# Order of SyncE's queue in an adaLN layer: the spread of 1/std one slot later, the loads of x behind the norm

## The chip, the cores and the metric

The kernel runs on one core of a Trainium2 chip. The metric is the device time of one execution in microseconds (us), as a median over runs. The engines are named as the profile does: PE (TensorE matmuls; PEld its weight loads), DVE (VectorE), ACT (ScalarE), POOL (GpSimd), SP (SyncE). SyncE computes nothing here. It issues nearly all DMAs, in the order of the program, and each issue first waits for what that DMA needs.

## The reference

One layer on `x` of shape (4, 2048, 512), float32: a state-space part and a channel-mixing part, each behind a layer norm and with a gate, modulated by a small input `c`. Cut to what matters:

```python
mod = (_silu(c) @ wmod).reshape(4, 6, 1, -1)              # sa, ca, ga, sb, cb, gb
h = _layernorm(x) * (1 + ca) + sa
omega = clip(softplus(h @ W_omega.T + b_omega)); zeta = sigmoid(h @ W_zeta.T + b_zeta)
A, S, d, F = omega**2, 1 / (1 + DT*DT*omega**2), 1 - zeta, h @ W_B.T + b_B
# scan over the 2048 tokens, 2 x 64 states:
z, y = d*(S*z - DT*A*S*y) + F_z,  d*(DT*S*z + S*y) + F_y
x = x + ga * (states @ C.T + h @ D_mat.T)
h = _layernorm(x) * (1 + cb) + sb
xr, xk = (mu * h + (1 - mu) * h_prev_token for mu in (mu_r, mu_k))
x = x + gb * sigmoid(xr @ W_r.T) * (square(relu(xk @ W_k.T)) @ W_v.T)
```

The norm needs a mean and a standard deviation for each of the 8192 tokens. Its scale 1/std multiplies the gate projections token by token, and there the tokens lie along the free dimension. So the kernel needs each unit's 1/std as a row on all 128 partitions.

## The kernel before

**Units and slots.** The tokens are cut into 32 units of 256 tokens. Unit number i belongs to batch row i % 4 and to token stretch i // 4. Four units with the same stretch form a block, and the scan over tokens runs block by block. The main loop (L1205) has one slot per unit. In slot i several units are at different stages:

- `fin[i]` (class `Finish`) does its key product (`key_fast`), its receptance product (`receptance_fast`) and its `value`, and its results go out (L760).
- `fin[i+1]` (`ahead` in the code) gets its direct product with `dg` and the states, its statistics (`stats`, L557 and L559), its norm, and its mixing (`mix`).
- `fin[i+2]` is loaded (`x`, L117; `xt`, L114).
- `gts[i+8]` (class `Gates`) is projected (`project_pieces`, L244), multiplied by its spread 1/std (`multiply`, L252) and delivered to the scan.
- `gts[i+9]` gets its norm: means (L186) and squares (L192) on ScalarE, then 1/std and std on GpSimd (L196 to L198).
- `gts[i+10]` has its two tiles of `x` loaded (`load`, L159; the tiles are called `xs`).

`at = i % 4` is the place of a slot in its block. I call `at == 0` the first slot and `at == 3` the fourth. Slots below i = 4 have a branch of their own that the change does not touch. In the slots from i = 4, the norm's ScalarE work stands between the products of the key multiplication, except in the first slot. There it stands behind `deliver`, almost at the slot's end, because ScalarE also has the scan's functions to do in that slot.

**How a norm reaches the gates.** `send` (L202) writes a unit's std and 1/std from `rs` (SBUF) to a small DRAM tile `st`: 512 numbers, 2 KB. `spread` (L213) reads the row of 1/std back onto all 128 partitions, into `bc`. A spread therefore waits for the landing of its send. The scan reads the rows of std from the same DRAM tiles (`load_std`, L408, in a block's third slot).

**Buffers that matter.** `xs` has three buffers and a unit takes two. So of the two loads for `gts[i+10]` one finds a free buffer, and the other has to wait until the squares of `gts[i+9]` are done. `xt` has three buffers, shared by `fin` and `gts`. `r` (the receptance, and then the result that goes out) has two buffers, one for each half of a unit. The first and second eviction of a receptance product (L666 and L669, both on ScalarE) write the two `r` buffers, so they have to wait until the results of the previous unit have left. The third of the seven receptance products accumulates in the bank that L666 reads, so TensorE waits for L666. `bc` has two buffers.

**What sets the order.** Each engine runs its instructions in the order in which this Python code emits them. The order is written out by hand: `f.emit(products, beside)` emits the seven products of a multiplication and, behind each, the jobs listed for it. For the SyncE queue the order within a slot is therefore the order in which `load`, `send`, `spread`, `fetch` and `value` are called in the code. `fetch("dg", i + 3)` and `fetch("wv", i + 2)` bring a batch row's 1 MB weights back from DRAM (L800).

Of the kernel before, what the change touches and what calls it, by code (L numbers as in the profile page):

```python
# [22 lines left out]
B, T, D, M = 4, 2048, 512, 64  # L23
# [24 lines left out]
def adaln_layer_kernel(ctx: ExitStack, tc: tile.TileContext, x, x_t, c_t, wmod, w_gate, w_b, b_gate, b_f, c_mat, d_mat,  # L48
# [99 lines left out]
    class Gates:  # L148
# [62 lines left out]
        def spread(self, queue=nc.sync):  # L211
            self.bc = p2.tile([P, W], F32, tag="bc", name=f"bc_{self.u.tag}")
            queue.dma_start(self.bc, self.rows[0:1, :].broadcast_to([P, W]))  # L213
# [582 lines left out]
    def fetch(name, i):  # L796

        if 6 <= i < len(fin):
            dst = dg if name == "dg" else wvb
            nc.sync.dma_start(dst[:, i % 2].rearrange("p k d -> p (k d)"), kept[name][i % B])  # L800
# [404 lines left out]
    for i, f in enumerate(fin):  # L1205
        at = i % B
        ahead = fin[i + 1] if i + 1 < len(fin) else None
        if i < 4:
            if i == 3:
                take(100)  # L1210
            fin[i + 2].load()
            gts[i + 10].load()
            f.key()
            if i < 2:
                rows(turn_d[i + 2], turn_c[i + 2])
            if i == 0:
                gts[6].multiply()
                gts[6].deliver(share=2)
            else:
                norm_send(i + 9)  # L1220
            if i == 3:
                gates(11)
            take(6)
            if i == 2:
                sums_s(key_weights, quarters_of(wk, True))
            if i == 3:
                sums_t(receptance_weights, quarters_of(wr))
            ahead.attend(lambda: take(2))
            ahead.normalize()
            turn(turn_v[i])  # L1230
            keep_in_dram("wv", i)
            if i == 3:
                fetch("dg", i + 3)
            if i == 0:
                gts[7].multiply()
                gts[7].deliver(share=2)
                gts[8].norm_dve()
                gts[8].send()
                gts[8].spread()
                gts[9].norm_dve()  # L1240
                gts[9].send()
            if i == 1:
                gates(9)
            if i:
                take(5)
            f.receptance()
            ahead.mix(fin[i + 2].shift)
            if i == 0:
                side += scan(1)
                take(0.1)  # L1250
                take(0.1)
            gts[i + 9].load_t()
            gts[i + 9].spread()
            if i < 3:
                turn_v[i + 1].rows()
            f.value(lambda: take(3 if i == 0 else 4))
            if i < 2:
                turn(turn_d[i + 2], turn_c[i + 2])
                keep_in_dram("dg", i + 2)
                gates(8 if i == 0 else 10)  # L1260
        else:
            if i + 2 < len(fin):
                fin[i + 2].load()
            shares = [0] * 7
            if at < B - 1:
                left = sum(e[1] for e in side if e) if at == B - 2 else 1
                shares = [e * left for e in SHARES[at]]
            scans = [lambda e=e: take_share(e) for e in shares]

            def fill(jobs, n):  # L1270
                for _ in range(n):
                    if jobs:
                        jobs.pop(0)()

            def filler(jobs, n):
                return lambda: fill(jobs, n)

            direct, ends = ahead.attend_pieces() if ahead else ([[], []], [])
            gate = gts[i + 8].project_pieces() if i + 8 < len(gts) else []

            def stats(n, part=None):
                return lambda: ahead.stats(n, part) if ahead else None

            def finish_norm():
                if ahead:
                    ahead.normalize_rest()

            def norm_means():
                if i + 9 < len(gts):
                    gts[i + 9].norm_means()  # L1290

            def norm_squares():
                if i + 9 < len(gts):
                    gts[i + 9].norm_squares()
                    gts[i + 9].send()

            def load_gates():
                if i + 10 < len(gts):
                    gts[i + 10].load()

            if at < B - 1:
                load_gates()
            eight = i in EIGHT
            if not eight:
                f.receptance_sums()

            if not ahead:
                one, other = f.key_fast(), f.receptance_fast((ps1, "pg"))
                f.emit(one[:2])
                for n in range(2, len(one)):  # L1310
                    f.emit(one[n : n + 1])
                    f.emit(other[n - 2 : n - 1])
                    if n == 5:
                        f.relu(1)
                        f.squares(1)
                f.relu(0)
                f.squares(0)
                f.emit(other[5:])
                finish = None
            elif at == B - 1:  # L1320
                take(100)
                take(1)
                load_gates()
                d = direct[0] + direct[1]
                fill(d, 2)
                f.emit(f.key_fast(), {1: [filler(d, 1), norm_means], 7: [filler(d, 1), norm_squares], 6: [filler(d, 1)], 4: [filler(d, 1)],
                            5: [filler(d, 1)], 2: [filler(d, 1)]})
                fetch("dg", i + 3)
                f.relu(0)
                fill(ends, 1)  # L1330
                stats(0)()
                fill(ends, 1)
                stats(1)()
                f.relu(1)
                finish = {1: [filler(gate, 1), lambda: f.squares(0)], 7: [filler(gate, 1)],
                          6: [filler(gate, 1), finish_norm], 4: [filler(gate, 1), lambda: f.squares(1)]}
            else:
                scans[0]()
                d = direct[0] + ends[:1] + direct[1] + ends[1:]
                fill(d, 2)  # L1340

                acts = ([lambda: take(0.1), lambda: take(0.1)], [norm_means, norm_squares])[at > 0]
                acts = acts + [lambda: None] if at != 1 else [lambda: None] + acts
                f.emit(f.key_fast(), {1: [filler(d, 2)], 7: [filler(d, 1), acts[0]],
                                      6: [filler(d, 2), scans[1], acts[1], stats(0)],
                                      4: [filler(d, 2), scans[2], acts[2]], 5: [filler(d, 1), scans[3]],
                                      2: [stats(1, 0)], 3: [stats(1, 1), scans[4]]})
                fetch("dg", i + 3)
                finish = {1: [filler(gate, 1)], 7: [filler(gate, 1), lambda: f.relu(0)],
                          6: [filler(gate, 1), finish_norm],  # L1350
                          4: [filler(gate, 1), scans[5], lambda: f.relu(1), lambda: f.squares(0)],
                          5: [lambda: f.squares(1)]}
            if eight:
                for k in (1, 7, 6, 4, 5):
                    for job in finish.get(k, ()):
                        job()
                f.receptance()
            elif ahead:
                f.emit(f.receptance_fast(), finish)

            def between():
                if not eight:
                    f.sigmoids()
                if i + 2 < len(fin):
                    fin[i + 2].shift()

            if ahead:
                ahead.mix(between)
            else:
                f.sigmoids()  # L1370
            if i + 9 < len(gts):
                gts[i + 9].load_t()
            fill(gate, len(gate))
            if i + 8 < len(gts):
                gts[i + 8].multiply()
                gts[i + 8].deliver()
            if at == 0:
                norm_means()
                norm_squares()
            if i + 9 < len(gts):  # L1380
                gts[i + 9].spread()
            f.value(scans[6], parts=1 if ahead else 2)
            fetch("wv", i + 2)
        if at == B - 1 and i + 8 < len(gts):
            assert not side
            side += scan(i // B + 2)
# [43 lines left out]
```

## Time and profile before

| what | us |
|---|---|
| median of 3 runs | 1166.02 |
| lowest and highest run | 1164.06, 1168.04 |
| the profiled execution, its time | 1167.16 |
| its span in the profile | 1165.3 |
| TensorE busy in that span | 1108.0 |

The profile is of one execution. Its time is 1.86 us more than its span, which is what lies around the program's first and last instruction. A row of the engine view gives, for each engine, its busy time and the number of instructions. The rows of waits read "who waited, on which line, for whom: total us, how often, the longest". A row of the timeline gives start, duration, engine, line, operation, and in brackets how long the engine had been idle before and who ended that. DMA rows of SyncE (SPq) give the time of issue; several issues of one line that follow each other are merged into one row, whose duration then includes the waits between them.

### The profile page before, as it was taken

The page shows a single profiled execution, that of the slowest core. Times are in us where ns is not written, and L with a number is a line of the kernel's source. Part 1 is how long each engine was busy: PE and PEld are TensorE (multiplying, and loading weights), DVE is VectorE, ACT ScalarE, POOL GpSimd, SP SyncE. Part 2 cuts the span into 40 slices and gives each one's busy share as a digit, 9 for nine tenths or more (in the row PEclk, how much of TensorE's full clock was granted, in tenths as well). Part 3 has the DMA queues.
Part 4 walks back from the last instruction along what each step waited for, and adds up shares of the span by engine and source line. Part 5 has one row for each costly group of instructions (what it writes and reads, how often), then busy time and mean ns, then how long its engine had stood idle before and what let it go on. Part 6 is the DMA issues. An engine that isn't in the chain of part 4 may idle for free.

```text
span 1165.3 us, 14897 instructions
## 1 busy us (share of the span) xinstructions
PE 1108.0 (95%) x4772; PEld 747.4 (64%) x4772; DVE 777.8 (67%) x2158; ACT 669.3 (57%) x1380; POOL 188.9 (16%) x389
## 2 busy tenths in 40 slices
PE   7898899999899997999889998999979999999998
PEld 4556566656666665777566675666657765566666
DVE  5796678547576585756857566765867568764444
ACT  1655776638465675556666475656756465435553
POOL 1212201211111122101211111111221011111110
PEclk9889899999899998999999999999989999999999
DMA  9895374540787527883297825967168433443211
GB/s 299 304 153 143 89 161 141 153 158 6 193 177 180 146 64 170 179 167 118 65 257 143 157 76 166 199 177 155 62 165 168 145 127 127 136 145 127 91 55 37
DMA packets 133991, 168.32 MB, mean 144 GB/s; under 512 B 22292, under 2 KB 96788, under 8 KB 126104
## 3 DMA queue, kind: packets, MB, share of 16 engines
q1 hardware_dynamic: 130904, 166.03, 55.9%
q10 hardware_dynamic: 2688, 0.79, 0.3%
q8 instruction: 38, 0.62, 0.3%
q0 software_dynamic: 320, 0.53, 0.2%
q14 instruction: 41, 0.34, 0.1%
HBM read 137.90 MB, written 25.23 MB: 140 GB/s over the span
## 4 chain that ended last, share of the span: by engine, by line
PE 79%; DVE 12%; DMA 4%; ACT 4%; issue 1%; POOL 0%; ACTq 0%; DVEq 0%; POOLq 0%
PE pv_c L754 16%; PE pd_c L538 13%; PE pxr_c L657 8%; PE pxk_c L657 7%; PE pg L244 5%; PE pr_c L739 4%; PE pzk_c L657 3%; PE pzr_c L657 3%; PE pd_c L493 3%; PE pg L234 3%; PE pd_c L470 3%; PE pt_c L594 2%; DMA out_dram<-r_c 2%; PE pyr_c L657 2%; PE pk_c L627 2%; PE pyk_c L657 2%
## 5 line engine op out<-in xcount | busy, mean ns | idle before, releaser
L754 PE MATMUL pv_c<-wvb,act_c 128*128 128x512 f32 (+1 forms) x528 | 225.0, 580 | 0.0
L538 PE MATMUL pd_c<-dg,xt 128*128 128x512 f32 x432 | 206.2, 593 | 0.0
L603 DVE SCALAR_TENSOR_TENSOR mixed_c<-pt_c,prev_f,mixed_c 128x255 f32<-128x255 f32 x256 | 118.1, 481 | 80.9 <-ACT mixed_c L600 80.5
L754 PEld LDWEIGHTS pv_c<-wvb,act_c 128*128 128x128 f32 x528 | 99.6, 190 | 105.5 <-issue 100.1
L600 ACT ACTIVATE mixed_c<-pt_c,mod,now_f 128x256 f32<-128x256 f32 x256 | 130.2, 559 | 19.8 <-DVE mixed_c L603 14.0
L538 PEld LDWEIGHTS pd_c<-dg,xt 128*128 128x128 f32 x432 | 74.6, 191 | 55.9 <-issue 54.2
L244 PE MATMUL pg<-xt,wgb 128*128 128x256 f32 x320 | 89.0, 392 | 6.9 <-DMA xt<-in_x_t_dram 6.9
L478 DVE SCALAR_TENSOR_TENSOR x<-pd_c,rs,x 128x512 f32<-128x512 f32 x64 | 47.6, 745 | 54.0 <-PE pd_c L493 48.7
L657 PE MATMUL pxr_c<-wvb 128*128 128x256 f32 x208 | 58.6, 408 | 23.2 <-ACT r_c L666 23.2
L657 PEld LDWEIGHTS pxk_c<-dg 128*128 128x128 f32 x448 | 58.8, 192 | 25.9 <-issue 24.4
L244 PEld LDWEIGHTS pg<-xt,wgb 128*128 128x128 f32 x320 | 61.0, 197 | 15.8 <-issue 8.0
L463 POOL TENSOR_TENSOR x<-x,d 128x1024 f32<-128x1024 f32 x30 | 70.9, 2362 | 0.0
L557 ACT ACTIVATE xn_c<-x 128x512 f32<-128x512 f32 x44 | 27.7, 628 | 67.7 <-DVE x L478 63.9
L574 ACT ACTIVATE xn_c<-x,mean_c,var_c 128x512 f32<-128x512 f32 x64 | 48.6, 808 | 29.5 <-POOL mean_c L572 29.5
L267 ACT ACTIVATE pre<-g,bias 64x256 f32<-64x256 f32 x56 | 41.5, 742 | 37.6 <-DVE g L252 30.8
L657 PEld LDWEIGHTS pxr_c<-wvb 128*128 128x128 f32 x208 | 41.3, 203 | 31.4 <-ACT r_c L666 25.6
L657 PE MATMUL pxk_c<-dg 128*128 128x128 f32 x448 | 59.1, 275 | 0.0
L675 DVE TENSOR_TENSOR r_c<-r_c,pzr_c 128x256 f32<-128x256 f32 x26 | 10.9, 420 | 69.4 <-PE pzr_c L657 35.9
L493 PE MATMUL pd_c<-cg,y 128*128 128x512 f32 x112 | 56.5, 595 | 0.0
L606 POOL TENSOR_TENSOR mixed_c<-mixed_c,edge_c 128x4 f32<-128x4 f32 x64 | 12.9, 201 | 263.5 <-ACT mixed_c L600 263.4
L757 DVE TENSOR_TENSOR r_c<-pv_c,r_c 128x512 f32<-128x512 f32 (+1 forms) x66 | 44.0, 666 | 9.6 <-PE pv_c L754 9.6
L758 DVE TENSOR_TENSOR r_c<-r_c,x 128x512 f32<-128x512 f32 (+1 forms) x66 | 44.6, 676 | 2.3
(261 smaller groups left out, 2135.4 us busy)
## 6 DMA issues: line engine op xcount, KB each, us to landing
dg<-dg SPq DMA_DIRECT2D x30, 1024.0 KB, 5.8
xt<-in_x_t_dram SPq DMA_DIRECT2D x116, 256.0 KB, 7.5
wvb<-wv SPq DMA_DIRECT2D x26, 1024.0 KB, 5.5
x<-in_x_dram SPq DMA_DIRECT2D x32, 512.0 KB, 6.7
out_dram<-r_c SPq DMA_DIRECT2D x62, 256.0 KB, 2.2
xs<-in_x_dram SPq DMA_DIRECT2D x54, 256.0 KB, 6.8
wvb<-in_wmod_dram SPq DMA_DIRECT2D x5, 1024.0 KB, 8.6
y<-pre SPq DMA_DIRECT2D x64, 64.0 KB, 4.6
```

The lines of the kernel that those rows point to most:

```text
L244: nc.tensor.matmul(self.pg[:, i, :], wgb[:, u.b, k, ts(i, P)], self.xt[:, k, :], start=(k == 0), stop=(k == KC - 1))
L463: engine.tensor_tensor(xt, xt, d0[:, self.u.b, :].unsqueeze(1).broadcast_to([P, NT, D]), ALU.add)
L478: nc.vector.scalar_tensor_tensor(xt, pd, r, xt, ALU.mult, ALU.add)
L493: nc.tensor.matmul(pc, y_of[u.s][:, u.b, ts(n, P)], cg[:, u.b, :], start=start, stop=True)
L538: nc.tensor.matmul(pds[n], self.h[:, k, ts(n, P)], dg[:, self.at, k, :], start=(k == 0), stop=False)
L574: nc.scalar.activation(self.xn[:, n, :], self.x[:, n, :], AF.Identity, bias=self.mean[:, n : n + 1], scale=self.var[:, n : n + 1],)
L600: nc.scalar.activation(m, pt, AF.Identity, bias=mod[:, SB, k, b : b + 1], scale=now_f[:, b, i, k : k + 1])
L603: nc.vector.scalar_tensor_tensor(m[:, 1:], pt[:, : W - 1], prev_f[:, b, i, k : k + 1], m[:, 1:], ALU.mult, ALU.add)
L657: nc.tensor.matmul(to[:, j, :], left[:, k, ts(j, P)], right[:, k, :], start=start and j == k == 0, stop=(k == 1), skip_group_check=True,)
L739: nc.tensor.matmul(pr, mixed[:, 0, k, ts(n, P)], wr[:, k, :], start=(k == 0), stop=(k == KC - 1))
L754: nc.tensor.matmul(pv, act[:, k, ts(n, P)], wvb[:, self.at, k, at], start=(j == 0), stop=(j == KC - 1))
L758: nc.vector.tensor_add(r[:, at], r[:, at], xt[:, n, at])
```

## The change

The program's arithmetic is the same, and so is the order of instructions on TensorE, VectorE, ScalarE and GpSimd. What moves is the place of three kinds of DMA in SyncE's queue, in the slots from i = 4:

- The spread: slot i used to spread `gts[i+9]`, shortly before `value`. It now spreads `gts[i+8]`, the unit that this same slot multiplies, behind the key product. Slot 4 spreads nothing, since slot 3 has spread its unit already.
- The loads of `xs` for `gts[i+10]`: they stood at the slot's start (in the fourth slot behind the scan's last jobs). They now follow the send of `gts[i+9]` directly.
- The send: in the second, third and fourth slot it used to be issued inside the key product, right behind the squares. It now stands behind the key product, and in the second and third slot behind the fetch of `dg`. In the first slot it used to follow the squares, ahead of the spread and of the results; it now stands behind both results of `value`, with the loads behind it.

```diff
             def norm_squares():
                 if i + 9 < len(gts):
                     gts[i + 9].norm_squares()
+
+            def send_load():
+                if i + 9 < len(gts):
                     gts[i + 9].send()
+                load_gates()
 
             def load_gates():
                 if i + 10 < len(gts):
                     gts[i + 10].load()
 
-            if at < B - 1:
-                load_gates()
+            def spread():
+                if 4 < i < len(gts) - 8:
+                    gts[i + 8].spread()
+
             eight = i in EIGHT
...
             elif at == B - 1:
                 take(100)
                 take(1)
-                load_gates()
                 d = direct[0] + direct[1]
                 fill(d, 2)
                 f.emit(f.key_fast(), {...})
+                send_load()
+                spread()
                 fetch("dg", i + 3)
...
                 fetch("dg", i + 3)
+                if at:
+                    send_load()
+                spread()
                 finish = {...}
...
             if at == 0:
                 norm_means()
                 norm_squares()
-            if i + 9 < len(gts):
-                gts[i + 9].spread()
             f.value(scans[6], parts=1 if ahead else 2)
+            if at == 0:
+                send_load()
             fetch("wv", i + 2)
```

## The prediction

> **What bounds the kernel now.** I read the page's first two parts, then the same row per slot, then who ends TensorE's waits, then SyncE's queue.
>
> ```profile
> PE 1108.0 (95%) x4772; PEld 747.4 (64%) x4772; DVE 777.8 (67%) x2158; ACT 669.3 (57%) x1380; POOL 188.9 (16%) x389
> ...
> core 0: us, PE busy (x) PEld busy (x) DVE busy (x) ACT busy (x) POOL busy (x), PEclk, DMA share, GB/s
> 287.10:328.40 41.30, 36.31 (x145) 24.60 (x145) 28.20 (x81) 23.76 (x54) 7.69 (x14) 0.88 0.63 164
> ...
> 529.20:561.30 32.10, 32.10 (x146) 22.33 (x145) 20.69 (x45) 22.44 (x43) 5.24 (x11) 1.00 0.27 90
> 561.30:602.00 40.70, 33.98 (x145) 23.15 (x145) 28.19 (x81) 23.76 (x54) 7.68 (x14) 0.96 0.64 161
> 602.00:634.10 32.10, 32.10 (x145) 22.18 (x145) 25.03 (x92) 20.03 (x45) 5.43 (x11) 1.00 0.81 170
> ```
>
> The windows run from the end of one slot's `value` matmuls to the next one's. TensorE fills a normal slot: 32.1 us busy of 32.1. The second slot of a block does not fit that. The five windows of this kind (287.1, 424.6, 561.3, 698.3, 834.6) last 41.3, 40.4, 40.7, 40.0 and 40.3 us, 42.2 us in all above 32.1 each. 30.1 us of that is idle TensorE (length less busy), the other 12.1 us mostly half clock after it (PEclk 0.88 to 0.96). So these 42.2 us are all that a reordering can win here. Who ends the wait:
>
> ```profile
> PE pxr_c L657 <- ACT r_c L666: 23.2, 5, 6.4
> PE pg L244 <- DMA xt<-in_x_t_dram: 6.9, 3, 3.5
> ...
> ACT r_c L666 <- DMA out_dram<-r_c: 37.9, 5, 8.1
> ...
> SPq L213 <- DMA st<-rs: 196.1, 22, 12.2
> SPq L159 <- ACT xs L192: 172.6, 12, 31.5
> ...
> 533.54 32.09 SPq L159 DMA_DIRECT2D xs<-in_x_dram  x2
> 565.73 0.38 SPq L800 DMA_DIRECT2D dg<-dg  x1
> 566.16 1.23 SPq L114 DMA_DIRECT2D xt<-in_x_t_dram  x2
> 567.88 0.38 SPq L202 DMA_DIRECT2D st<-rs  x1
> 579.24 0.33 SPq L213 DMA_DIRECT2D bc<-st  x1
> 579.65 0.86 SPq L760 DMA_DIRECT2D out_dram<-r_c  x2
> ```
>
> Five times ScalarE cannot write `r` (L666), because the last slot's results still have to leave that buffer. SyncE issues in order: a load of `xs` waits through the whole first slot for the norm, then the spread waits for the send (11.3 us), and only then do the results go, 15 us after VectorE made the second (L758 ended at 564.5). They land at 585.2, L666 starts at 585.25, TensorE at 585.68.
>
> **The change, part by part.** Work on TensorE, VectorE, ScalarE and GpSimd stays, in its order; SyncE's list alone is shuffled.
>
> *The spread a slot later.* Its 1/std was sent a slot earlier and has landed, so SyncE's 196.1 us of waiting go. The results of a first slot then go out when made (561.5 and 564.5) and land some 2.2 us later, ten before `r` is written. The 37.9 us of ScalarE's wait go.
>
> *`dg` and `xt` of a first slot.* Both go up to 20 us earlier; the 6.9 us of TensorE's wait for `xt` go.
>
> *Results first, then send, then loads, at the end of a first slot.* The send still needs GpSimd's 1/std, so it stays at 567.88. Both loads of `xs` now follow it, at about 568.3 and 568.7; before, one was issued 35 us earlier and the other at 565.30. Their reader is the next slot's norm, early in ScalarE's list:
>
> ```profile
> 568.30 0.37 ACT L672 COPY act_c<-pxk_c 128x256 f32<-128x256 f32 x1 [1.38 <-PE pxk_c L657]
> 568.57 0.63 ACT L186 ACTIVATE xs<-xs 128x512 f32<-128x512 f32 x1
> ...
> 572.25 0.63 ACT L557 ACTIVATE xn_c<-x 128x512 f32<-128x512 f32 x1 [2.35 <-DVE x L478]
> ...
> 576.44 0.72 ACT L559 ACTIVATE xn_c<-x,mean_c 128x512 f32<-128x512 f32 x1
> ...
> 585.25 0.37 ACT L666 COPY r_c<-pxr_c 128x256 f32<-128x256 f32 x1 [8.00 <-DMA out_dram<-r_c]
> ```
>
> Queued behind L186 are the statistics of the next unit, the squares, the last eviction of the key product and L666 itself, for which TensorE's third receptance product waits. From L186 to L666 there are 1.34 us (568.57 to 569.91) and 5.00 us (572.25 to 577.25), less 0.21 us of waiting for TensorE: 6.13 us of work, and TensorE resumes 0.43 us after. So the question is X, the time from the send to the landing of the first `xs`.
>
> No `xs` load follows a send in this trace. Nearest are the third slots, where `dg` (1024 KB) follows a send on a queue with little ahead: sends at 339.73, 476.00, 612.98, 749.28 and 885.02; `dg` issued 0.63 to 1.17 us later lands 12.3, 14.0, 13.7, 13.5 and 13.7 us after its issue, thus 13.2, 14.9, 14.4, 14.1 and 14.9 us after the send, mean 14.3. Alone, `dg` takes 5.0 to 5.2 us and an `xs` 2.6; the smaller load is 2.5 us quicker, so X is 11.8 us. From below: a send alone lands after 8.9 us at the earliest, and some 0.7 us of transfer follow: 9.6. From above: the four `std` loads behind the send at 200.13, 256 KB together, landed by 13.2. I take 11.8, the row nearest in place and load.
>
> Here two statements of the Trainium skill pull apart. Its page "DMA: Bandwidth & Descriptors", section "Anatomy of one DMA — SWDGE (gpsimd) path", fits a DMA of that path as 2.0 us plus bytes over 436 GB/s: 2.6 us for 256 KB, which the trace shows on SyncE's queue too when nothing is ahead. By that X is about 3, ScalarE's 2.35 us of slack swallows the wait, and the sum is the full gain of 42 us. The section "Queues, rings and completion order" says that a semaphore's increment lands only after all earlier writes of that DMA engine, and the send's writes are just ahead. It speaks against this change, and the third slots are on its side, with X four times as long. I go by the row.
>
> Per block: L666 can start at send + 11.8 + 6.13, plus 0.17 because the second tile lands some 0.8 us after the first while its activation is ready 0.63 us after. That is send + 18.1. Before it was send + 17.43, 16.65, 17.37, 16.46, 16.76 (L666 at 311.09, 447.83, 585.25, 721.33, 857.94), mean 16.93. The stall is thus kept and grows by 1.2 us: five times, +5.9 us.
>
> *The clock.* The first of the five windows lost 4.2 us beyond its idle time, the others about 2 each, with PEclk 0.88 against 0.92 to 0.96. The page "TensorE: Matmul & The Clock Gate", section "What's actually happening", has the clock halved after an idle window of about 3.4 us and full after a busy one. By that, one cold window per stall costs 1.7 us, 3.6 us less than before's 12.1 over five. By the rows, only the first comes down to the others' 2: -2.0 us. I take the rows.
>
> *Loads and spread of the other slots.* In the second slot the norm is done at send + 16.3 and GpSimd 1.74 us later, so the next send goes at 585.9. Its loads land by 599 and are read at 607.6: no cost. The spread behind them lands between 599.0 (scaled from `dg` for 640 KB ahead and with it) and 602.4 (3.4 us more, since a spread's median landing is 6.0 us where an `xs` alone has 2.6). `multiply` wants it at 599.12 plus the shift, 599.8. VectorE may thus wait up to 2.6 us; ScalarE's 1.79 us of idle time before 604.63 and TensorE's bank, wanted only at 603.5, cover nearly all. I put 0, at most +0.5 per block. In third and fourth slots the spread is out by 627 and 523, wanted at 631 and 526: no cost while sends stay within 4 us of the present.
>
> Sum: +5.9 - 2.0 = +3.9 us. The profiled execution (span 1165.3, time 1167.16) stands 1.1 us above the median 1166.02; from it the sum is 1171.1, from the median 1170, which I forecast. 0.3% (3.5 us) is about what a measurement of this kernel can tell from no change.
>
> **The rivals.**
>
> *The loads land early (faster).* Each us of X is 5 us in all, and the change breaks even at X = 11.0. Between 9.6 and 11.0 it wins 0 to 7 us (to 1159). For it: the queue is emptier before the moved send than in most others, and a lone send took 8.9. If the loads pass the send's small writes altogether, X is about 3 and all 42 us go: 1124. Against that: all `dg` loads behind a send took 12.3 us and more from their issue.
>
> *The wait is dearer (slower).* X near 13.2, as with `std`, gives +10.9; with `wv`, `x` and `xt` (2 MB) pressing behind, a colder clock, and the late spread at +0.5, up to +17: 1183. For it: sends with much beside them took up to 14.0 us.
>
> *The change does not free the results.* Only if another wait held SyncE before L760; I see none in a first slot.
>
> **How the numbers follow.** X from 11.0 to 13.2, the moved stall: 0.60 (a quarter of it within 0.3%). X from 9.6 to 11.0: 0.16, half of it within 0.3%. Loads that pass the send: 0.06. The dearer wait: 0.18. So faster 0.14, same 0.23, slower 0.63. The range 1159 to 1183 leaves out the 0.06 and about a third of the dear case.
>
> **What would show it.** Right: ScalarE's wait for `out_dram` gone, in its place L186 waiting for DMA `xs`, five times by 10 to 12 us; second-slot windows of 40 to 43 us, all others 32.1; SyncE's L213 without waits. Wrong: L186 starting within 3 us of L672 and second slots of 32 to 35 us (the loads passed), a window other than the five above 33 us (a cover failed), or L666 still waiting for `out_dram`.

## The result and the profile after

The changed kernel takes 1177.51 us (median of 4 runs, 1176.74 to 1181.17), the kernel before 1165.05 us on the same chip: a ratio of 1.0109 (95% interval 1.008 to 1.0138), or 12.5 us more. A second series of both gave 1180.54 against 1166.94 us, ratio 1.0132 (1.011 to 1.0153). The profiled execution took 1181.17 us, the highest of its four, with a span of 1179.4 us. That is 14.0 us more than the profiled execution of before.

First the row per slot of the changed kernel. The columns are the length of the stretch, the busy time of PE, PEld, DVE, ACT and POOL, then the granted clock, the DMA share and GB/s. The first five rows are the second slots of the five blocks, then come a third slot and the one other slot that grew:

```profile
PE 1110.8 (94%) x4772; PEld 749.8 (64%) x4772; DVE 778.3 (66%) x2158; ACT 668.0 (57%) x1380; POOL 184.7 (16%) x389
...
285.50:329.30 43.80, 35.08 (x145) 24.11 (x144) 28.12 (x81) 23.37 (x54) 6.80 (x14) 0.88 0.54 123
425.60:469.10 43.50, 35.27 (x145) 24.29 (x144) 27.99 (x79) 23.37 (x54) 6.79 (x14) 0.88 0.48 124
565.40:609.00 43.60, 35.39 (x145) 24.34 (x145) 28.18 (x81) 23.43 (x54) 6.79 (x14) 0.88 0.58 124
705.30:749.00 43.70, 35.34 (x145) 24.31 (x144) 28.08 (x79) 23.21 (x54) 6.78 (x14) 0.88 0.58 124
845.80:888.90 43.10, 35.41 (x145) 24.36 (x145) 28.04 (x80) 23.46 (x54) 6.78 (x14) 0.88 0.52 126
609.00:641.10 32.10, 32.10 (x145) 22.16 (x144) 25.05 (x93) 20.02 (x45) 5.43 (x11) 1.00 0.64 161
781.10:813.70 32.60, 32.31 (x146) 22.35 (x145) 19.07 (x48) 17.29 (x37) 5.00 (x10) 1.00 0.53 166
```

The same five slots stall as before, and each is longer: 217.7 us together against 202.7, so +15.0. One other slot (781.1) grew by 0.5 us, and the start of the program was 1.6 us shorter, which is the remainder: +14.0. The waits (who waited, on which line, for whom: total us, times, longest) name the new cause:

```profile
POOL var L196 <- ACT xs L192: 270.1, 25, 22.8
...
ACT xs L186 <- DMA xs<-in_x_dram: 60.4, 9, 12.1
...
PE pxr_c L657 <- ACT r_c L666: 41.2, 5, 8.7
...
SPq L213 <- DMA st<-rs: 25.9, 3, 11.2
```

ScalarE's 37.9 us for `out_dram` at L666 and TensorE's 6.9 us for `xt` are gone, and SyncE's wait for the send fell from 196.1 us to 25.9. The waits that remain lie at the program's start, before the slot i = 4. In their place stands L186, the first instruction of the norm, which waits for the loads of `xs`. TensorE still waits for L666, now for 41.2 us instead of 23.2 + 6.9. SyncE's queue and ScalarE in the second slot that began at 565.4:

```profile
565.65 3.36 SPq L760 DMA_DIRECT2D out_dram<-r_c  x2
571.98 0.38 SPq L202 DMA_DIRECT2D st<-rs  x1
572.40 0.97 SPq L159 DMA_DIRECT2D xs<-in_x_dram  x2
573.47 0.38 SPq L800 DMA_DIRECT2D wvb<-wv  x1
```

```profile
572.39 0.37 ACT L672 COPY act_c<-pxk_c 128x256 f32<-128x256 f32 x1 [1.38 <-PE pxk_c L657]
584.20 0.63 ACT L186 ACTIVATE xs<-xs 128x512 f32<-128x512 f32 x1 [11.43 <-DMA xs<-in_x_dram]
...
585.53 0.63 ACT L186 ACTIVATE xs<-xs 128x512 f32<-128x512 f32 x1 [0.62 <-DMA xs<-in_x_dram]
...
590.61 0.35 ACT L666 COPY r_c<-pxr_c 128x256 f32<-128x256 f32 x1
```

The results leave at once, as meant. The send goes at 571.98, and the loads right behind it. They land 12 us after the send, although SyncE has only 2 KB in front of them. ScalarE then works without a gap from the second L186 to L666, so the landing of `xs` sets the stall. The send's own row of landings (issue to landing) has the same length:

```profile
L202 SPq DMA_DIRECT2D st<-rs x24: 377/381/1323, 129.7 to 900.6; - x24
...
DMA to landing us min/median/max: 8.7/11.7/13.4
```

### The profile page after: what moved, and what is told of

The parts are those of the page before. It is cut to its first block, busy times and chain, and to the rows that moved or that the text cites. A ratio compares the mean times of both kernels' runs of the same rounds, so it can differ in the third digit from the quotient of the medians.

```text
span 1179.4 us, 14906 instructions
## 1 busy us (share of the span) xinstructions
PE 1110.8 (94%) x4772; PEld 749.8 (64%) x4772; DVE 778.3 (66%) x2158; ACT 668.0 (57%) x1380; POOL 184.7 (16%) x389
## 4 chain that ended last, share of the span: by engine, by line
PE 76%; ACT 9%; DMA 8%; DVE 4%; issue 2%; POOL 1%; SPq 0%; ACTq 0%; DVEq 0%; POOLq 0%
PE pv_c L754 15%; PE pd_c L538 12%; PE pxr_c L657 8%; PE pxk_c L657 6%; DMA xs<-in_x_dram 5%; PE pg L244 5%; PE pzr_c L657 4%; PE pr_c L739 4%; PE pzk_c L657 3%; PE pd_c L493 3%; PE pd_c L470 3%; PE pg L234 3%; PE pt_c L594 2%; PE pyr_c L657 2%; PE pk_c L627 2%; PE pyk_c L657 2%
## 5 line engine op out<-in xcount | busy, mean ns | idle before, releaser
L657 PE MATMUL pxr_c<-wvb 128*128 128x256 f32 x208 | 60.5, 418 | 41.2 <-ACT r_c L666 41.2
L657 PEld LDWEIGHTS pxk_c<-dg 128*128 128x128 f32 x448 | 58.7, 192 | 25.9 <-issue 24.4
L186 ACT ACTIVATE xs<-xs 128x512 f32<-128x512 f32 x52 | 32.3, 623 | 60.8 <-DMA xs<-in_x_dram 60.4
L196 POOL TENSOR_SCALAR var<-var 128x2 f32<-128x2 f32 x26 | 8.0, 306 | 270.2 <-ACT xs L192 270.1
```

What stands on the lines that cost most here:

```text
L657: nc.tensor.matmul(to[:, j, :], left[:, k, ts(j, P)], right[:, k, :], start=start and j == k == 0, stop=(k == 1), skip_group_check=True,)
```

## The experiments

Two questions were open: whether the loads' place behind the send is all that costs, and why a 2 KB write delays 256 KB loads by 10 us. Each ratio below is against the kernel before, run on the same chip.

### Which part of the change does what

**The loads ahead of the send.** In the first slot alone, the two loads of `xs` go out ahead of the send. Edit against the changed kernel:

```diff
             if at == 0:
-                send_load()
+                load_gates()
+                if i + 9 < len(gts):
+                    gts[i + 9].send()
```

> The changed kernel, but at the end of each first slot the two loads of xs stand ahead of the send instead of behind it. Theory (the small writes of the send hold back the landing of every DMA issued behind them): both loads are issued 2 to 3 us ahead of the send and land 2.6 to 3 us after their issue, ScalarE waits at L186 for under 1.5 us, the second slots fall from 43.6 us to 32 to 34 us, and the time to 1122 to 1135 us. A load issued about 1 us ahead of a send landed 12 us later in three first slots of the kernel before; if that catches the second tile, 1150 to 1177 us. Rival (the loads are late because they go out at the slot's end with 2 MB of wv, x and xt right behind them, and the send has no part in it): they are issued only 3 us earlier, so 2 to 3 us per block are won, 1160 to 1166 us.

Measured: 1129.58 us, ratio 0.9726 (0.9707 to 0.9745). L186 no longer waits, L666 starts 9.26 us after the send in every block (18.66 on average in the changed kernel), and the five second slots last 32.07 to 32.08 us. So the whole stall of the second slots was the loads' place behind the send. What is left has moved on, as the waits of this kernel show:

```profile
DVE g L252 <- DMA bc<-st: 24.5, 6, 5.2
...
PE pxk_c L657 <- DVE r_c L757: 5.7, 4, 2.1
```

In the second slot the spread now goes out behind that slot's send, and lands late for `multiply` (L252). Four third slots last 33.4 to 34.5 us.

**The spread alone.** The kernel before, with the spread a slot later. The send keeps its place. In the first slot the loads of `xs` go behind the spread; in the other slots they stay. The edit, without the fourth slot's spread:

```diff
+            def spread():
+                if 4 < i < len(gts) - 8:
+                    gts[i + 8].spread()
+
-            if at < B - 1:
+            if 0 < at < B - 1:
                 load_gates()
...
                 fetch("dg", i + 3)
+                spread()
+                if at == 0:
+                    load_gates()
...
-            if i + 9 < len(gts):
-                gts[i + 9].spread()
             f.value(scans[6], parts=1 if ahead else 2)
```

> The kernel before with one part of the change alone: the spread a slot later. The send stays right behind the squares, so in a first slot it goes out 0.4 us ahead of the results; the loads of xs stay at the slot's start, except that in a first slot they stand behind the spread. Theory: the results, issued right behind the send, land some 12 us after it instead of 2.2 us after their own issue. L666 starts at send + 12.5 to 13 us, against 16.9 in the kernel before: second slots of 36 to 37 us, 1142 to 1150 us. Rival (only SyncE's wait for the send held the results; what stands behind a send lands as usual): results land at send + 3 us, L666 does not wait, second slots of 32 to 33 us, 1122 to 1128 us.

Measured: 1137.08 us, ratio 0.978 (0.9751 to 0.9808). SyncE doesn't wait for the send any more. But the results now stand right behind the send (550.80, then 551.28), and L666 starts 11.5 to 12.6 us after it, since it still waits for them:

```profile
ACT r_c L666 <- DMA out_dram<-r_c: 11.9, 4, 3.3
```

The second slots last 33.5 to 34.6 us. The send thus delays whatever stands behind it, here the results, in the changed kernel the loads. The changed kernel's other part, moving the sends and the loads, turned a gain of 2.2% into a loss of 1.1%.

### Why a write of 2 KB holds the loads

**The send in pieces of 16 bytes.** As it stands, the send writes 512 pieces of 4 bytes.

```diff
-                self.rows.rearrange("i (n p) -> p (i n)", p=P),
+                self.rows.rearrange("i w -> (i w)").rearrange("(p e) -> p e", p=P),
```

> The changed kernel with the send written as 128 pieces of 16 bytes instead of 512 of 4 bytes, the same 2 KB to the same DRAM tile. The numbers then lie in another order in the tile, so each token is scaled with another token's 1/std and std; nothing else is changed. Theory (it is the number of small writes that takes the send's time): the send and the load behind it land after 4 to 7 us instead of 12.2, ScalarE's wait at L186 falls from 11.4 to 3 to 6 us, 1130 to 1150 us. Rival (a fixed latency of the send, or the traffic behind it): X stays 11 to 12 us and the time 1170 to 1178 us.

Measured: 1118.45 us, ratio 0.963 (0.9616 to 0.9644), with the changed kernel's order of the queue. Landings of the sends, and ScalarE's wait:

```profile
DMA to landing us min/median/max: 1.4/2.7/6.4
```

```profile
ACT xs L186 <- DMA xs<-in_x_dram: 21.0, 5, 4.5
```

L186 starts 4.9 to 5.3 us after the send, and the second slots last 32.6 to 33.0 us. The 2 KB and the order stayed, only the pieces changed: the pieces make the delay. (This kernel is a probe and no replacement: `spread` and the scan read the tile in the old order, so each token gets another token's numbers.)

**Two sends in a row.** If the pieces were worked off one by one, twice as many should take twice as long. A second send of the same data, to a place that nobody reads, stands between the send and the loads; the changed kernel ran again on the same chip.

```diff
             if at == 0:
-                send_load()
+                if i + 9 < len(gts):
+                    gts[i + 9].send()
+                    g = gts[i + 9]
+                    again = dram.tile([2, W], F32, ...)
+                    nc.sync.dma_start(again..., rs[:, g.u.b, g.u.s]...)
+                load_gates()
```

> The changed kernel with the send of each first slot issued twice, the second time to a DRAM tile that nobody reads; the loads of xs follow both. Theory (the engines work off the 4-byte writes one after the other, and the loads behind them land when that is done): 512 more writes take about as long as the first 512, so the loads land 20 to 23 us after the first send instead of 12.4, each second slot grows by 8 to 11 us, and the time to 1217 to 1232 us. Rival (a fixed latency of a send that two of them share): X grows by under 2 us, 1177 to 1187 us.

> The changed kernel itself, on the same chip as the three next to it. Every theory: 1.0 to 1.4% above the kernel before, 1172 to 1182 us, ScalarE waiting at L186 for DMA xs five times by 11 to 12 us.

Measured: 1181.98 us (ratio 1.0141, 1.0122 to 1.016) against 1180.54 for the changed kernel. L186 starts 13.2 to 14.2 us after the first send, against 12.8 to 13.5 without the second. Two sends share nearly the whole time, so the theory of a serial count of small writes fell.

**The send on another queue.** GpSimd issues the send of the first slot, SyncE a write of 8 bytes as a mark where the send stood, and the loads behind it.

```diff
+                if i + 9 < len(gts):
+                    gts[i + 9].send(nc.gpsimd)
...
-                send_load()
+                if i + 9 < len(gts):
+                    g = gts[i + 9]
+                    mark = dram.tile([1, 2], F32, ...)
+                    nc.sync.dma_start(mark, rs[0:1, g.u.b, g.u.s, 1, :])
+                load_gates()
```

> The changed kernel, but GpSimd issues the send of a first slot on its own queue, as soon as it has made std. On SyncE's queue a write of 8 bytes stands in its place, so that the loads of xs go out at the same time as in the changed kernel. Theory in its narrow form (only what stands behind the send in the same queue is held): xs lands 2.6 to 4 us after its issue, ScalarE's wait at L186 falls to under 4 us, 1120 to 1128 us. In its wide form (the DMA engines' writes are held across queues): the wait stays 8 to 12 us, 1160 to 1182 us.

Measured: 1164.8 us, ratio 0.9984 (0.9966 to 1.0001). In one second slot GpSimd issued the send at 568.69, and SyncE the loads from 568.73 on:

```profile
568.83 0.37 ACT L672 COPY act_c<-pxk_c 128x256 f32<-128x256 f32 x1 [1.38 <-PE pxk_c L657]
571.52 0.63 ACT L186 ACTIVATE xs<-xs 128x512 f32<-128x512 f32 x1 [2.31 <-DMA xs<-in_x_dram]
...
578.71 0.63 ACT L186 ACTIVATE xs<-xs 128x512 f32<-128x512 f32 x1 [6.47 <-DMA xs<-in_x_dram]
```

The first tile passed, the second, issued a little later on the other queue, was held by 4.9 to 9.6 us. So another queue is no way out. The page "DMA: Bandwidth & Descriptors" of the Trainium skill, section "Queues, rings and completion order", says that a semaphore increment lands only after every earlier write of that DMA engine, across its queues. The second tile agrees with it. The first agrees if the send's writes reached the DMA engines only after that load, which no view here shows. The section doesn't say why those writes take 10 us.

**How the pieces lie in DRAM.** Four kernels answer that. All are built on the best version below, whose own send comes later, behind the loads of `x` and `xt`, in all four alike. Where the changed kernel has its send they have a write of the same data to a place that nobody reads, and behind it the loads of `xs`. They differ in the number of pieces of 4 bytes and in the distance between two pieces in DRAM.

```diff
+                if i + 9 < len(gts):
+                    g = gts[i + 9]
+                    again = dram.tile([4 * P, 1], F32, ...)     # dense; [4 * P, 16] spaced, [4 * P, 4] one in 16 bytes
+                    nc.sync.dma_start(
+                        again.rearrange("(e p) o -> p (e o)", p=P),   # again[:, 0:1] where spaced
+                        rs[:, g.u.b, g.u.s].rearrange("p i n -> p (i n)"),
+                    )
                 load_gates()
# a quarter: again is [P, 1], written from rs[:, g.u.b, g.u.s, 1, 0:1]
```

> Late-send kernel (1121) with one more write, of the send's shape, where the changed kernel has its send: 512 pieces of 4 bytes, side by side in DRAM (16 of them in each 64 bytes), into a place that nobody reads. The loads of xs stay behind it. Both theories: the loads are held as in the changed kernel, ScalarE's L186 waits 11 to 13 us in the five second slots, these last 42 to 44 us and the time is 1172 to 1183. If L186 waits under 5 us (below 1140), then it was not this write that held them, but something else at that point.

> As the kernel with the dense write, but each of the 512 pieces of 4 bytes goes to a 64-byte stretch of DRAM of its own: count, size and the engines' share are the same, only the neighbourhood in DRAM differs. Theory A, pieces that fall on the same stretch of DRAM wait for one another: L186 waits 2 to 5 us, the second slots last 32.1 to 33, 1121 to 1140. Theory B, each piece of 4 bytes is slow wherever it goes: L186 waits 11 to 13 us and the time is 1172 to 1183, as dense.

> As the kernel with the dense write, but with a quarter of the pieces: 128 of 4 bytes, side by side, one from each partition. Theory A, neighbours in the same stretch of DRAM wait for one another (16 per 64 bytes, as dense): L186 waits 9 to 12 us, 1160 to 1180. Theory B, the latency goes with the number of pieces: a quarter of it beyond the 2.6 us of a lone load, L186 waits 4 to 6 us, 1121 to 1135. If L186 waits under 3 us, then 128 pieces of 4 bytes hold nothing.

> As the kernels with the dense and the spaced write, 512 pieces of 4 bytes, but one in every 16 bytes of DRAM: 4 in each 64 bytes, where the dense write has 16 and the spaced one has 1. If the latency goes with the number of pieces in the same small stretch: between the two (landing 2.2 us spaced, 10.4 dense), near the write in pieces of 16 bytes, which also has 4 per 64 bytes and landed after 2.7 us at the median: L186 waits 3 to 5.5 us, 1121 to 1132. If it goes with how many bytes lie between the first and the last piece (2 KB dense, 8 KB here, 32 KB spaced), or if every shared stretch costs the full price: L186 waits 8 to 11 us and the time is 1155 to 1175.

| write | pieces in each 64 bytes | landing, min/median/max us | write to L186, us | time, us | ratio (95%) |
|---|---|---|---|---|---|
| dense, 512 pieces | 16 | 9.4/10.4/11.7 | 11.8 to 12.3 | 1171.91 | 1.0081 (1.0051 to 1.0111) |
| dense, 128 pieces | 16 | 7.6/8.2/8.7 | 10.3 to 11.4 | 1163.99 | 1.0016 (1.0005 to 1.0028) |
| one in 16 bytes, 512 pieces | 4 | 2.9/3.3/3.6 | 4.5 to 5.3 | 1125.78 | 0.969 (0.9663 to 0.9717) |
| one in 64 bytes, 512 pieces | 1 | 2.1/2.2/2.2 | 3.7 to 4.9 | 1122.85 | 0.9654 (0.9619 to 0.9689) |

The rows for the dense and then for the spaced write of 512 pieces, each with its landings:

```profile
L1397 SPq DMA_DIRECT2D again<-rs x5: 377/377/377, 291.7 to 845.0; - x5
...
DMA to landing us min/median/max: 9.4/10.4/11.7
```

```profile
L1397 SPq DMA_DIRECT2D again<-rs x5: 377/377/378, 289.5 to 803.4; - x5
...
DMA to landing us min/median/max: 2.1/2.2/2.2
```

Same queue, same 512 pieces, same data, and 2.2 us against 10.4. A quarter of the pieces, packed as closely, still takes 8.2. So it is not their 4 bytes that make the delay, and only in a small part their number, but how many share a small stretch of DRAM. (The 2 KB as a whole is not such a stretch: the send in pieces of 16 bytes fills the same 2 KB and lands after 2.7.) The time follows: 49 us lie between the spaced and the dense write. The page named above says under "Specifications" that transfers below 512 B are done by reading, changing and writing back. Sixteen such writes to one stretch that wait for one another would look like these rows, but that this is the mechanism, and how long a stretch is, no run here shows. Every piece here is below 512 B, spaced or dense, so that rule alone does not tell the rows apart. Whether it matters that several of the 16 DMA engines write to one stretch was not tried.

### What is left, and the best version

**The send late.** The loads of `xs` go behind the results at the end of the first slot, with no send ahead of them. The send moves to the start of the second slot, behind the loads of `x` and `xt`, where the next readers have time.

```diff
             if i + 2 < len(fin):
                 fin[i + 2].load()
+            if at == 1 and i + 8 < len(gts):
+                gts[i + 8].send()
...
             if at == 0:
-                send_load()
+                load_gates()
```

> The changed kernel, but the send of a first slot is moved to the start of the second slot, behind its loads of x and xt; the loads of xs stay at the first slot's end, behind the results. Nothing small is ahead of or right behind the loads of xs, and the 2 MB of wv, x and xt follow them as before. Theory: xs lands 2.6 to 3.5 us after its issue, L186 waits under 1.5 us, second slots of 32 to 33 us unless the spread now comes too late for L252 (which then waits up to 3 us), 1122 to 1132 us. Rival (traffic behind the loads): like the first kernel's rival, 1160 to 1166 us.

Measured: **1121.46 us, ratio 0.965 (0.9631 to 0.967)**, 40.9 us below the kernel before on this chip (1162.35). A second slot and the third behind it, and what is left of the wait for the spread:

```profile
543.00:575.10 32.10, 32.10 (x146) 22.33 (x146) 28.04 (x80) 22.56 (x52) 7.70 (x14) 1.00 0.75 169
575.10:607.20 32.10, 32.10 (x146) 22.19 (x145) 25.17 (x91) 20.06 (x44) 5.43 (x11) 1.00 0.61 160
```

```profile
DVE g L252 <- DMA bc<-st: 6.0, 3, 3.6
```

All second, third and fourth slots of the five blocks now last 32.07 to 32.15 us, and TensorE is busy throughout.

**The spread ahead of the send.** The other way to mend the first experiment: its order in the first slot, and in the later slots the spread ahead of that slot's send (shown for the fourth slot; likewise in the second and third).

```diff
-                send_load()
                 spread()
+                send_load()
```

> The kernel with the loads ahead of the send (1129.6 us), and in the slots after the first also the spread ahead of the send and the loads. There VectorE waited 24.5 us at L252 for the spread behind a second slot's send. Theory: the spread now lands before it is wanted, this wait goes but for the start of the kernel (under 8 us), third slots fall from 33.4 to 34.5 us to 32.1, 1119 to 1125 us. Rival (the spread is late because its own send went out only a slot ago): the wait and the 1129 us stay.

Measured: 1132.18 us, ratio 0.9725 (0.9697 to 0.9753); the expected gain did not come. The spread first waits for the landing of its own send, which is late itself, and so is issued only 0.5 to 1.4 us ahead of the next send (565.75 and 567.16 in one slot). That is too little, and it is held too:

```profile
DVE g L252 <- DMA bc<-st: 23.4, 5, 5.4
```

Its third slots last up to 36.4 us. In the five second slots such a spread landed 8 to 14 us after its issue, where the quickest spread of this kernel took 3.5. The loads of the first experiment, issued 1.5 to 2.9 us ahead of a send, did pass.

## Why the prediction was right

It forecast 1170 us, slower, within 1159 to 1183; the median is 1177.5. The moved stall came as described, but the sum was far too small: +3.9 us, where +12.5 came. The result lies inside the range because the range had room for the rival of the dearer wait. Several sizes were off, and for the clock the sign.

- **What the move frees.** Right: `out_dram`, `xt` and SyncE's waits at L213 went as written, and the results landed long before L666.
- **The loads behind the send keep the stall.** Right, with L186 as the new wait. Undoing that step alone (the first experiment) removes the stall entirely.
- **X, send to first `xs`.** Taken as 11.8 us; measured 12.77, 12.86, 12.22, 12.06 and 12.04, mean 12.4 (13.1 in the repeat). The row of the third slots, `dg` behind a send, was the right one to go by; the 2.5 us subtracted from its 14.3 for the smaller load were too many, 1.9 (1.2 in the repeat) would have been right. The fit by bytes, about 3 us, is nearer to what the spaced write measures (3.7 to 4.9), where little holds the loads.
- **The second tile.** Taken as 0.17 us late; its activation starts 0.71 to 1.64 us after the first, mean 1.19 where 0.63 is the least. That is 0.56.
- **ScalarE from L186 to L666.** Taken as 6.13 us of work. Without its gaps it is 5.7. So L666 starts at 12.4 + 0.56 + 5.7 = 18.66 us after the send, where 18.1 was forecast and 16.93 measured before: five times 1.73, +8.6 us, not +5.9.
- **The clock.** Taken as -2.0 us; here the sum failed most. From L666 to the end of the slot the five slots took 6.4 us more than before (15.0 less 8.6), on the same matmuls. The rows of slots cut in two at L666 (columns as in the row per slot, so the third value from the end is the granted clock), first of the kernel before (both parts of the first block, then the second part of the third):

```profile
287.10:311.09 23.99, 19.42 (x88) 12.96 (x87) 19.09 (x55) 11.60 (x32) 4.82 (x10) 0.88 0.38 113
311.09:328.40 17.31, 16.89 (x57) 11.64 (x58) 9.11 (x26) 12.15 (x23) 2.87 (x4) 0.87 0.97 236
...
585.25:602.00 16.75, 16.32 (x57) 11.24 (x58) 9.08 (x26) 12.14 (x23) 2.86 (x4) 0.90 0.97 234
```

  then the second part of the third block in the changed kernel:

```profile
590.61:609.00 18.39, 17.98 (x57) 12.38 (x58) 9.10 (x26) 12.03 (x25) 4.10 (x8) 0.82 0.59 110
```

  Behind L666 TensorE was busy for 16.3 to 16.9 us in the five slots before, and for 17.7 to 18.0 us in the changed kernel. The prediction had compared whole slots, and wanted to win back 2 of the 4.2 us that the first one lost. But these 2 us lay ahead of L666 (19.42 us busy there, 17.4 to 17.7 in the other blocks), inside the stall, where they delayed nothing. So that gain was not there to be had.

  What was lost behind L666 depends on when TensorE resumes. Half clock came in stretches of 3.41 us, or of two or three times that. The first stretch in which TensorE worked again, in the third block, before:

```profile
585.11:588.52 3.41, 2.84 (x7) 2.31 (x8) 0.00 (x0) 2.00 (x5) 0.00 (x0) 0.50 1.01 415
```

  and in the changed kernel, with the stretch behind it:

```profile
590.36:593.78 3.42, 2.76 (x7) 2.23 (x8) 0.00 (x0) 2.06 (x7) 1.31 (x5) 0.50 1.07 354
593.78:597.19 3.41, 3.41 (x10) 2.69 (x9) 0.42 (x1) 2.69 (x5) 0.00 (x0) 0.50 1.09 56
```

  Before, half clock ended with the first of these, busy for 2.84 of 3.41 us. In the changed kernel 2.76 us were not enough, and a whole further stretch stayed at half clock. TensorE resumed at 591.02 and had full clock from 597.19: 6.2 us at half clock, so 3.1 us lost. All five stalls of the changed kernel went like this (2.8 to 3.1 us lost); before, 1.4 to 2.0 us were lost. The page "TensorE: Matmul & The Clock Gate", section "What's actually happening", has full clock after one busy window of about 3.4 us. These rows agree with it if 2.76 us of work do not make a window busy. The prediction's 1.7 us per stall by that page counted one window, and left out the rest of the one in which TensorE resumes.
- **Spread and loads elsewhere.** Taken as 0; one slot grew by 0.5 us. Right.
- **Sum.** +3.9 forecast; +8.6 + 6.4 + 0.5 - 1.6 = +13.9 in the profile, against +14.0 between the two profiled executions and +12.5 between the medians.

Of the rivals, the early loads did not come (no X below 12.0), and the results were freed. The dearer wait had the direction of the error: X between 11.8 and its 13.2, and a colder clock. The bound of 42.2 us on what a reordering can win held too: the best order won 40.9. The send in pieces of 16 bytes won 43.9, but it also shortens the start, which no reordering touched: its first slot ended at 131.0, those of the other kernels at 136.5 to 140.6.

## What to carry to other kernels

Before a transfer that is needed soon is moved behind a small write, read the landing of the nearest DMA that already stands behind such a write; the trace had it here, and its own size told nothing. A scattered write of single elements belongs behind everything whose reader is close, on whatever queue, or into larger pieces. And where a stall is only exchanged for one of about the same length, price the clock after it anew, and only behind the instruction that ends the stall; it took 6.4 of 15 us here.

## What the runs showed of the hardware

- A DMA of 512 pieces of 4 bytes that lie side by side in DRAM landed after 10.4 us; one piece in every 16 bytes took 3.3 us, one in every 64 bytes 2.2 us. 128 pieces side by side took 8.2 us.
- It holds loads behind it on its own queue, and on another one the second of two loads. A DMA issued 0.5 to 1.4 us ahead of it can be held too: in the kernel before, three `xt` loads issued 1.1 us ahead of a first slot's send landed 11.6 to 13.6 us after their issue. But two spreads of the last experiment, issued 0.7 us ahead, landed after 3.5 and 5.1 us. Two such writes in a row delayed the loads only by 0.2 to 1.1 us more than one (means 13.8 and 13.1).
- Half clock lasted 10.24 us at each of the five stalls of the changed kernel, including the stretch in which TensorE still waited, and 3.4 to 10.2 us in the kernel before. In these two traces, the repeat and the four variants that stall likewise (two sends, another queue, dense, a quarter), it ended at all 35 stalls with the first stretch of 3.41 us in which TensorE was busy for 83% or more; after stretches of 81% or less it went on. This holds for these stalls only: at the start of the kernel before, a stretch busy throughout did not end it.
- The half clocks of the five stalls of the changed kernel begin 139.9 us apart, which is 41 such stretches, so all five met the stretches at nearly the same point (TensorE busy for 66 to 81% of the one in which it resumed). What a shift against them would save was not tried.
